# Spreading the output product's four matmuls between the last projection products of a step

## The chip, the cores and the metric

The kernel runs on one core of one Trainium2 chip. The metric is the device time of one execution in microseconds (us); a run of the kernel is timed several times and the median is given. The engines of the core are TensorE (PE in the profile; PEld is its weight load), VectorE (DVE), ScalarE (ACT), GpSimd (POOL) and SyncE (SP, which issues transfers). Each works through its own list of instructions in order and waits on semaphores for the others.

## The reference

The input x has 128 rows (S) of 256 tokens (R) of 256 channels, all float32. Two layers follow each other, each adding its result to x. Layer 0, which the change is in, works on the group-normalized x:

```python
gate = jax.nn.sigmoid(msa_repr @ gate_proj).reshape(bs, s, r, head, c)
q, k, v = jnp.split(msa_repr @ qkv_proj, 3, axis=-1)
sim = jnp.einsum('nsqhc,nskhc->nshqk', q, k) * scale
sim = jax.nn.softmax(sim, axis=-1)
sim = sim + bias
attend = jnp.einsum('nshqk,nskhc->nsqhc', sim, v) * gate
out = attend.reshape(bs, s, r, cm) @ out_proj
```

Each of the 128 rows has its own attention over its 256 tokens, with 8 heads of 32 channels. The bias comes from the pair representation and is the same for all rows. The last line is the output product that the change moves. Layer 1 normalizes again and applies an attention with 4 heads within a band of 16 tokens.

## The kernel before, in words

Channels lie on the partitions (two halves of 128) and tokens along the free dimension. The kernel first reads x and the pair representation for the statistics and the bias, then runs layer 0 row by row, then layer 1.

In layer 0 the order on TensorE, ScalarE and VectorE is the order of the program text, written out by hand (`tc.manual_schedule`); only GpSimd's and the transfers' order is left to the framework's scheduler. The loop runs over steps s = 0 to 128. One step holds, on TensorE: the scores of row s for the first four heads (`scores(s, 0)`, tile sim, L640), the sums of the exponentials of row s-1 (`sum_heads`, zs, L681, and the bias product bv, L667), the scores of the other four heads, the weighted values of row s-1 (`attend`, av, L667), a `stretch` of projections for later rows, and the output product of row s-1 (`by_channel`, po, L513).

A stretch computes two of the four projections q, k, v, g for a pair of rows: q and k in an even step, v and g in an odd one, from s = 0 to 125. The first row pair's stretches stand ahead of the loop. Each projection is made by seven half-size products in the manner of Strassen (class `Seven`). Products 1, 5, 2, 3, 6, 7, 4 of the two projections f and g alternate. The products 3, 6, 7 and 4 build on each other in a projection's PSUM bank: 6, 7 and 4 accumulate in half 0, and ScalarE takes a snapshot of it after 6 and after 7 (`take("6")` L623, `take("7")` L625, each 128x256 to the tile mid) and of the whole bank at the end (`take("34")`, L627). A product may not write on until the snapshot before it has been taken. For v a product is two matmuls of 128 columns (L614), for q, k and g one of 256 columns (L610). A float32 matmul shows as two matmul records in the profile.

The snapshots are added up on GpSimd (L630, L631). GpSimd also makes the sums of rows that the products 4 to 7 read (`sum_rows`, L584 to L587, tile ts), once per row pair. VectorE normalizes (xt L503, xn L573), adds up exponentials (both, L657), and makes the reciprocal of the gated denominators (d, L696 and L697), from which the operand of the output product results:

```python
nc.vector.tensor_tensor(t, bv0, z, ALU.mult)
nc.vector.tensor_tensor(t, av, t, ALU.add)
at = row.tile([P, 2, R], F32, tag="at", name=f"at{s}")
nc.vector.tensor_tensor(at, t, d, ALU.mult)
```

`finish` then adds po to the row (o, L723). Scores, projections and output product share a ring of five PSUM banks; zs, bv and av have one bank each.

Of the kernel before, what the change touches and what calls it, by code (L numbers as in the profile page):

```python
# [15 lines left out]
P = 128  # L16
# [23 lines left out]
def conv_preact_kernel(  # L40
# [14 lines left out]
    nc = tc.nc  # L55
# [16 lines left out]
    def bank(which, name):  # L72
        pool, tag, bufs = ring[which]
        return pool.tile([P, 2, R], F32, tag=tag, name=name, bufs=bufs)

    def proj_bank(name):
        return bank("proj", name)
# [30 lines left out]
    out_sb = const.tile([P, 2, C], F32, name="out_sb")  # L108
# [399 lines left out]
    def by_channel(w, col, xn, name, ring="proj"):  # L508

        ps = bank(ring, name)  # L510
        for m in range(2):
            for kt in range(2):
                nc.tensor.matmul(  # L513
                    ps[:, m, :], lhsT=w[:, kt, col + m * P : col + (m + 1) * P], rhs=xn[:, kt, :],
                    start=(kt == 0), stop=(kt == 1),
                )
        return ps
# [14 lines left out]
    def rows(ap, s0, n):  # L532
        return ap[s0 : s0 + n].rearrange("s h p q -> p s h q")
# [5 lines left out]
    with ExitStack() as both:  # L539
# [11 lines left out]
        with ExitStack() as lay0:  # L551
            row = lay0.enter_context(tc.tile_pool(name="row0", bufs=2))
            att = lay0.enter_context(tc.tile_pool(name="att0", bufs=2))
            st, hd, outs = {}, {}, {}
# [5 lines left out]
            def normal(s):  # L560
                if s >= S:
                    return
                g, k = ROWS[s]
                if k == 0:
                    load(g + 1)
                xt = row.tile([P, 2, R], F32, tag="xt", name=f"xt{s}", bufs=6)
                turned(xt, xgs[g], k)
                st[s] = {"xt": xt}
                i, r = divmod(s, 2)
                if r == 0:  # L570
                    xns[i] = row.tile([P, 4, R], F32, tag="xn", name=f"xn{i}")
                for half in range(2):
                    nc.vector.tensor_scalar(  # L573
                        xns[i][:, 2 * r + half, :], xt[:, half, :],
                        mean0[:, half : half + 1], rstd0[:, half : half + 1],
                        op0=ALU.subtract, op1=ALU.mult,
                    )

            def sum_rows(i):

                if 2 * i >= S:
                    return
                x, t = xns[i], row.tile([P, 4, R], F32, tag="ts", name=f"ts{i}", bufs=1)
                nc.gpsimd.tensor_tensor(t[:, 0], x[:, 2], x[:, 0], ALU.subtract)  # L584
                nc.gpsimd.tensor_tensor(t[:, 1], x[:, 3], t[:, 0], ALU.subtract)
                nc.gpsimd.tensor_tensor(t[:, 2], x[:, 3], x[:, 2], ALU.subtract)
                nc.gpsimd.tensor_tensor(t[:, 3], t[:, 1], x[:, 1], ALU.subtract)  # L587
                tss[i] = t
# [44 lines left out]
            def scores(s, half):  # L633
                i, r = divmod(s, 2)
                q, k = res["q", i], res["k", i]
                sims = [sim_bank(f"sim{s}_{half}_{j}") for j in range(4)]
                for kt in range(2):
                    for j in range(4):
                        p0 = D0 * j
                        nc.tensor.matmul(  # L640
                            sims[j][:, kt, :],
                            lhsT=k[p0 : p0 + D0, 2 * r + half, kt * P : (kt + 1) * P],
                            rhs=q[p0 : p0 + D0, 2 * r + half, :],
                            start=True, stop=True,
                        )
                ex = att.tile([P, 4, 2, R], F32, tag="ex", name=f"ex{s}_{half}", bufs=4)
                both = att.tile([P, 4, R], F32, tag="both", name=f"both{s}_{half}")
                hd[s, half] = (ex, both)

                for j in range(4):  # L650
                    nc.scalar.activation(ex[:, j], sims[j], AF.Exp, scale=1.0 / math.sqrt(D0))  # L651
# [21 lines left out]
            def sum_heads(s):  # L673
                if s < 0:
                    return
                zs = ps_av.tile([P, 2, R], F32, tag="z", name=f"zs{s}")
                bv0 = ps_av.tile([P, 2, R], F32, tag="bv", name=f"bv{s}")
                for half in range(2):
                    both = hd[s, half][1]
                    for j in range(4):  # L680
                        nc.tensor.matmul(  # L681
                            zs[D0 * j : D0 * (j + 1), half, :], lhsT=ones[:, 0:D0], rhs=both[:, j, :],
                            start=True, stop=True,
                        )
                products(bv0, s, lambda h, kt: bias_sb[:, kt, h, :])
                hd[s] = bv0
                return zs
# [27 lines left out]
                nc.vector.tensor_tensor(at, t, d, ALU.mult)  # L715
                st[s]["at"] = at

            def finish(s, po):
                g, k = divmod(s, XG)
                if k == 0:  # L720
                    outs[g] = big1.tile([P, XG, 2, R], F32, tag="o", name=f"o{g}")
                o = outs[g]
                nc.vector.tensor_tensor(o[:, k], po, st[s]["xt"], ALU.add)  # L723
                if k % 2 == 1:
                    for half in range(2):
                        nc.vector.bn_stats(out=stats1[:, half, s // 2, :], in_=o[:, k - 1 : k + 1, half, :])
                if k == XG - 1:
                    nc.sync.dma_start(out=rows(x1, g * XG, XG), in_=o)
                    outs.pop(g)
                st.pop(s)  # L730

            def stretch(names, i):

                if 2 * i >= S:
                    return
                f, g = (Seven(w, i) for w in names)


                for p in (f, g):
                    p.open()  # L740
                    p.product(1)
                    p.product(5)
                    p.take("15")
                twos = proj_bank(f"p2{names}{i}")
                two = row.tile([P, 2, R], F32, tag="two", name=f"two{names}{i}")
                f.product(2, twos[:, 0, :])
                g.product(2, twos[:, 1, :])
                nc.scalar.copy(two, twos)  # L748
                for p in (f, g):
                    p.product(3)  # L750
                    p.product(6)
                    p.take("6")
                for p in (f, g):
                    p.product(7)
                    p.take("7")
                for p in (f, g):
                    p.product(4)
                    p.take("34")
                for n, p in enumerate((f, g)):
                    p.add(two[:, n, :])  # L760


            with tc.manual_schedule(engines={mybir.EngineType.PE, mybir.EngineType.Activation, mybir.EngineType.DVE}):
                for s in range(2):
                    normal(s)
                sum_rows(0)
                stretch("qk", 0)
                for s in range(2, 4):
                    normal(s)
                stretch("vg", 0)  # L770
                sum_rows(1)
                for s in range(S + 1):
                    if s < S:
                        scores(s, 0)
                    zs = sum_heads(s - 1)
                    join_tiles(s, 0, 0)
                    divide(s - 1, zs)
                    if s % 2 == 0 and s < S:
                        e = res["g", s // 2]
                        nc.scalar.activation(e, e, AF.Exp, scale=-1.0)  # L780
                    if s < S:
                        scores(s, 1)
                    z = hd[s - 1, "z"][0] if s > 0 else None
                    attend(s - 1)
                    for half, j in ((0, 2), (1, 0), (1, 2)):
                        join_tiles(s, half, j)
                    least(s - 1, z)
                    if s == S - 1:
                        most1 = join_most(st1, stats1, 1)
                        load1(0)  # L790
                        load1(1)
                    stretch(("qk", "vg")[s % 2], s // 2 + 1)
                    normal(s + 4)
                    if s % 2 == 1:
                        sum_rows((s + 3) // 2)
                    if s > 0:
                        finish(s - 1, by_channel(out_sb, 0, st[s - 1]["at"], f"po{s - 1}"))
            mean1, rstd1 = channel_columns(st1, most1, stats1, 1)
        banks0.close()

# [3 lines left out]
        with ExitStack() as lay:  # L804
# [3 lines left out]
            st, hd, outs = {}, {}, {}  # L808
# [362 lines left out]
```

## Time and profile before

| what | value |
|---|---|
| time, median of 3 runs | 3365.25 us (3362.61 to 3367.5) |
| span of the profiled execution | 3361.1 us |
| PE busy | 3268.2 us (97%), 37193 matmul records |
| PEld busy | 2493.9 us (74%) |
| DVE busy | 2685.3 us (80%) |
| ACT busy | 1818.2 us (54%) |
| POOL busy | 1254.2 us (37%) |
| po (L513): first and last start | 236.6 and 2183.3 us, 1024 records, median 379 ns |
| PE idle before po, until at was ready | 12.1 us, 3 times |

An engine's busy time is the sum of its instructions' durations as the profile gives them. Layer 0's loop runs from about 220 to 2185 us, so that its 128 steps take most of the time. In the profile's timeline each line has the start and the duration in us, the engine, the line of the kernel, the operation, what it writes and reads, and the shape; in square brackets stands the idle time of the engine ahead of it, and whom it waited for.

### The profile page before, as it was taken

How to read it: one execution, taken by the hardware profiler on the slowest of the kernel's cores; microseconds unless marked ns; L12 is line 12 of the kernel's file. 1: busy time of each engine (PE TensorE's matmuls, PEld its weight loads, DVE VectorE, ACT ScalarE, POOL GpSimd, SP SyncE). 2: the span in 40 equal slices, each digit the busy share in tenths (PEclk: the TensorE clock that was granted, in tenths of full speed). 3: DMA queues.
4: the chain of work that ended last, by engine and by line, in shares of the span. 5: the costliest groups of instructions: out<-in, count | busy, mean ns of one | idle time of the engine just before them, and what ended most of it. 6: DMA issues, size and time to landing. Idle time of an engine off the chain costs nothing.

```text
span 3361.1 us, 86626 instructions
## 1 busy us (share of the span) xinstructions
PE 3268.2 (97%) x37193; PEld 2493.9 (74%) x37193; DVE 2685.3 (80%) x3794; ACT 1818.2 (54%) x3866; POOL 1254.2 (37%) x1135
## 2 busy tenths in 40 slices
PE   6799999999999999999999999899999999999997
PEld 4566767666776767676767666588888888888886
DVE  4748988888888889888988888857777777777776
ACT  4566666666666666666666666444444444444442
POOL 3034344434444443444344434233333333333332
PEclk8899999999999999999999999999999999999998
DMA  9922111111111111111111111012222222222211
GB/s 383 410 69 58 45 39 33 39 33 33 39 36 35 33 39 33 39 33 39 33 39 33 39 33 27 20 33 62 55 65 64 53 64 64 60 57 64 64 52 46
DMA packets 346327, 209.35 MB, mean 62 GB/s; under 512 B 273608, under 2 KB 339152, under 8 KB 339664
## 3 DMA queue, kind: packets, MB, share of 16 engines
q1 hardware_dynamic: 345040, 201.37, 20.6%
q8 instruction: 294, 4.82, 0.6%
q0 software_dynamic: 752, 2.36, 0.2%
q14 instruction: 97, 0.79, 0.1%
q10 hardware_dynamic: 144, 0.00, 0.0%
HBM read 136.59 MB, written 67.11 MB: 61 GB/s over the span
## 4 chain that ended last, share of the span: by engine, by line
PE 92%; DMA 4%; DVE 2%; ACT 1%; issue 0%; ACTq 0%; SPq 0%; POOL 0%; DVEq 0%
PE sim L640 8%; PE p1v L835 7%; PE av L667 7%; PE 1po L513 7%; PE po L513 7%; PE p1q L513 7%; PE p1k L513 7%; PE bv L667 6%; PE pg L610 6%; PE pk L610 6%; PE pq L610 5%; PE pv L614 5%; PE zs L681 4%; PE 1sim L856 3%; PE 1avz L888 2%; DMA xs<-in_x_dram 2%
## 5 line engine op out<-in xcount | busy, mean ns | idle before, releaser
L651 ACT ACTIVATE ex<-sim 128x512 f32<-128x512 f32 x1024 | 528.8, 604 | 370.1 <-PE sim L640 370.1
L913 DVE RECIPROCAL 1rz<-1z 128x512 f32<-128x512 f32 x128 | 427.7, 3341 | 174.2 <-ACT 1z L911 174.2
L657 DVE TENSOR_TENSOR both<-ex 128x512 f32<-128x512 f32 x512 | 463.1, 944 | 113.0 <-ACT ex L651 113.0
L866 POOL TENSOR_TENSOR 1p<-1ex,seen 128x768 f32<-128x768 f32 x128 | 233.6, 1825 | 735.9 <-ACT 1ex L864 735.9
L697 DVE RECIPROCAL d<-d 128x512 f32<-128x512 f32 x128 | 429.2, 3353 | 4.4
L640 PE MATMUL sim<-q,k 32*128 32x256 f32 x4096 | 294.7, 400 | 1.1 <-ACT ex L651 1.1
L827 ACT ACTIVATE 1q<-p1q,bqk 128x256 f32<-128x256 f32 x256 | 107.2, 470 | 344.9 <-PE p1q L513 344.9
L630 POOL TENSOR_TENSOR v<-v,twovg 128x256 f32<-128x256 f32 x64 | 56.7, 886 | 592.8 <-ACT twovg L748 592.8
L640 PEld LDWEIGHTS sim<-q,k 32*128 32x128 f32 x4096 | 185.9, 184 | 102.2 <-issue 49.4
L513 PE MATMUL po<-at,out_sb 128*128 128x256 f32 x1024 | 245.6, 383 | 12.1 <-DVE at L715 12.1
L667 PE MATMUL av<-ex,v 128*32 128x256 f32 x4096 | 247.5, 382 | 0.0
L513 PE MATMUL 1po<-1at,w_out_t 128*128 128x256 f32 x1024 | 242.0, 390 | 5.0 <-DVE 1at L915 5.0
L513 PE MATMUL p1q<-xn,w_in_t 128*128 128x256 f32 x1024 | 243.7, 381 | 2.0 <-DVE xn L493 1.1
L667 PE MATMUL bv<-bias_sb,v 128*32 128x256 f32 x4096 | 244.5, 379 | 0.0
L513 PE MATMUL p1k<-xn,w_in_t 128*128 128x256 f32 x1024 | 241.9, 379 | 0.0
L835 PEld LDWEIGHTS p1v<-w_in_t,xn 128*64 128x64 f32 x4096 | 222.2, 137 | 21.6 <-issue 21.6
L835 PE MATMUL p1v<-w_in_t,xn 128*64 128x128 f32 x4096 | 237.9, 274 | 0.0
L513 PEld LDWEIGHTS 1po<-1at,w_out_t 128*128 128x128 f32 x1024 | 191.1, 192 | 54.9 <-ACT 1z L911 23.9
L513 PEld LDWEIGHTS po<-at,out_sb 128*128 128x128 f32 x1024 | 196.5, 192 | 40.5 <-issue 7.7
L513 PEld LDWEIGHTS p1q<-xn,w_in_t 128*128 128x128 f32 x1024 | 195.2, 191 | 29.4 <-issue 1.3
L513 PEld LDWEIGHTS p1k<-xn,w_in_t 128*128 128x128 f32 x1024 | 194.6, 190 | 26.5
L493 DVE TENSOR_SCALAR xn<-yg,mean,rstd 128x256 f32<-128x256 f32 x256 | 94.0, 410 | 138.7 <-PE p1v L835 138.7
(226 smaller groups left out, 6690.9 us busy)
## 6 DMA issues: line engine op xcount, KB each, us to landing
pr<-in_L_conv_pair_repr_dram SPq DMA_DIRECT2D x32, 1024.0 KB, 22.9
x<-o SPq DMA_DIRECT2D x64, 512.0 KB, 2.8
yg<-x SPq DMA_DIRECT2D x64, 512.0 KB, 4.2
out_dram<-1o SPq DMA_DIRECT2D x256, 128.0 KB, 4.1
xg<-in_x_dram SPq DMA_DIRECT2D x252, 128.0 KB, 3.1
xs<-in_x_dram SPq DMA_DIRECT2D x15, 2048.0 KB, 21.8
xs<-in_x_dram SPq DMA_DIRECT2D x2, 1024.0 KB, 17.9
qkv_sb<-in_L_conv_qkv_proj_dram POOLq DMA_DIRECT2D x4, 192.0 KB, 12.6
```

The source lines that it names most:

```text
L513: nc.tensor.matmul(ps[:, m, :], lhsT=w[:, kt, col + m * P : col + (m + 1) * P], rhs=xn[:, kt, :], start=(kt == 0), stop=(kt == 1),)
L610: nc.tensor.matmul(out, lhsT=stationary(self.w, n), rhs=moving, start=first, **flags)
L614: nc.tensor.matmul(out[:, cols], lhsT=moving[:, cols], rhs=stationary(self.w, n), start=first and t2 == 0, **flags)
L640: nc.tensor.matmul(sims[j][:, kt, :], lhsT=k[p0 : p0 + D0, 2 * r + half, kt * P : (kt + 1) * P], rhs=q[p0 : p0 + D0, 2 * r + half, :], sta ...
L651: nc.scalar.activation(ex[:, j], sims[j], AF.Exp, scale=1.0 / math.sqrt(D0))
L657: nc.vector.tensor_tensor(both[:, j : j + 2], ex[:, j : j + 2, 0, :], ex[:, j : j + 2, 1, :], ALU.add)
L667: nc.tensor.matmul(to[D0 * j : D0 * (j + 1), half, :], lhsT=v[:, 2 * r + half, c0 : c0 + D0], rhs=weights(4 * half + j, kt), start=(kt == ...
L681: nc.tensor.matmul(zs[D0 * j : D0 * (j + 1), half, :], lhsT=ones[:, 0:D0], rhs=both[:, j, :], start=True, stop=True,)
L697: nc.vector.reciprocal(d, d)
L835: nc.tensor.matmul(ps[KB * half : KB * (half + 1), b, :], lhsT=xn[:, kt, KB * b : KB * (b + 1)], rhs=w_in_t[:, kt, 2 * C + P * half : 2 * ...
L866: nc.gpsimd.tensor_tensor(p.rearrange("p j (r c) -> p (j r) c", c=WROW)[:, :, 0 : 2 * WSTEP] .rearrange("p r (t c) -> p r t c", c=WSTEP)[: ...
L913: nc.vector.reciprocal(rz, z)
```

## The change

The output product of row s-1 stood as a block of four matmuls after the stretch. It becomes a generator, `output(s)`, that gives out one matmul at a time. `stretch` gets the row as a third argument and takes one of the four matmuls between product 7 of f and product 7 of g, one between product 4 of f and product 4 of g, and the last two at its end. It is meant to give TensorE work in the places where a product waits for ScalarE's snapshot. Where there is no stretch (the last steps) the four stand together as before. `finish` reads the bank from the row's state. The computation is unchanged, and so is the number of instructions that compute.

```diff
-            def finish(s, po):
+            def finish(s):
+                if s < 0:
+                    return
+                po = st[s]["po"]
...
-            def stretch(names, i):
-
+            def output(s):
+
+                if s < 0:
+                    return
+                st[s]["po"] = proj_bank(f"po{s}")
+                for m in range(2):
+                    for kt in range(2):
+                        nc.tensor.matmul(
+                            st[s]["po"][:, m, :], lhsT=out_sb[:, kt, m * P : (m + 1) * P],
+                            rhs=st[s]["at"][:, kt, :],
+                            start=(kt == 0), stop=(kt == 1),
+                        )
+                        yield
+
+            def stretch(names, i, s):
+
+                po = output(s)
                 if 2 * i >= S:
+                    for _ in po:
+                        pass
                     return
...
-                for p in (f, g):
-                    p.product(7)
-                    p.take("7")
-                for p in (f, g):
-                    p.product(4)
-                    p.take("34")
+
+                for n, what in ((7, "7"), (4, "34")):
+                    f.product(n)
+                    f.take(what)
+                    next(po, None)
+                    g.product(n)
+                    g.take(what)
+                for _ in po:
+                    pass
...
-                    stretch(("qk", "vg")[s % 2], s // 2 + 1)
+                    stretch(("qk", "vg")[s % 2], s // 2 + 1, s - 1)
                     normal(s + 4)
                     if s % 2 == 1:
                         sum_rows((s + 3) // 2)
-                    if s > 0:
-                        finish(s - 1, by_channel(out_sb, 0, st[s - 1]["at"], f"po{s - 1}"))
+                    finish(s - 1)
```

The program's order on GpSimd, which the scheduler makes, changes too in the odd steps. Before: row sum L584, v plus mid, g plus mid, row sums L585, L586, L587. After: v plus mid, L584, L586, L585, g plus mid, L587.

More of the change, by code (lines that the diff above doesn't have):

```diff
@@ L766, in conv_preact_kernel @@
                 sum_rows(0)
-                stretch("qk", 0)
+                stretch("qk", 0, -1)
                 for s in range(2, 4):
                     normal(s)
-                stretch("vg", 0)
+                stretch("vg", 0, -1)
                 sum_rows(1)
```

## The prediction

> **What bounds the kernel now.** I read the page first (engine shares, then the chain that ended last), then the timeline of one step of layer 0 on the PE, weight-load, ScalarE and VectorE rows, then the windows view of two steps.
>
> ```profile
> PE 3268.2 (97%) x37193; PEld 2493.9 (74%) x37193; DVE 2685.3 (80%) x3794; ACT 1818.2 (54%) x3866; POOL 1254.2 (37%) x1135
> ...
> PE 92%; DMA 4%; DVE 2%; ACT 1%; issue 0%; ACTq 0%; SPq 0%; POOL 0%; DVEq 0%
> ```
>
> TensorE sets the time: 97% busy, 92% of the chain. But a matmul's end in the profile is modelled, so "busy" can hide loss. What counts is the distance between the starts of successive matmuls. The timeline of TensorE (start, duration, both in us) at the end of one q/k stretch:
>
> ```profile
> 1017.33 0.59 PE L610 MATMUL pk<-xn,sums_k 128*128 128x256 f32 x2
> 1017.76 0.59 PE L610 MATMUL pk<-ts,sums_k 128*128 128x256 f32 x2
> 1018.19 0.59 PE L610 MATMUL pq<-ts,sums_q 128*128 128x256 f32 x2
> 1018.81 0.70 PE L610 MATMUL pk<-ts,sums_k 128*128 128x256 f32 x2
> 1019.35 0.66 PE L610 MATMUL pq<-ts,sums_q 128*128 128x256 f32 x2
> 1019.98 0.70 PE L610 MATMUL pk<-ts,sums_k 128*128 128x256 f32 x2
> 1020.51 1.89 PE L513 MATMUL po<-at,out_sb 128*128 128x256 f32 x8
> 1022.33 1.15 PE L640 MATMUL sim<-q,k 32*128 32x256 f32 x16
> ```
>
> The first three starts are 0.43 apart. From product 7 of q (1018.19) on they are 0.62, 0.54, 0.63 and 0.53 apart: 2.32 us for four products where 4 x 0.433 = 1.73 would do. **0.59 us is lost per q/k step without an idle line to show it.** Why, is in the weight-load and ScalarE rows:
>
> ```profile
> 1018.01 0.37 PEld L610 LDWEIGHTS pq<-ts,sums_q 128*128 128x128 f32 x2
> 1018.81 0.30 PEld L610 LDWEIGHTS pk<-ts,sums_k 128*128 128x128 f32 x2 [0.43 <-ACT midk L623]
> 1019.31 0.30 PEld L610 LDWEIGHTS pq<-ts,sums_q 128*128 128x128 f32 x2 [0.20 <-issue]
> 1019.97 0.30 PEld L610 LDWEIGHTS pk<-ts,sums_k 128*128 128x128 f32 x2 [0.37 <-ACT midk L625]
> 1020.30 1.70 PEld L513 LDWEIGHTS po<-at,out_sb 128*128 128x128 f32 x8
> ```
>
> ```profile
> 1018.39 0.37 ACT L623 COPY midk<-pk 128x256 f32<-128x256 f32 x1 [0.49 <-PE pk L610]
> 1018.82 0.38 ACT L625 COPY midq<-pq 128x256 f32<-128x256 f32 x1
> 1019.55 0.37 ACT L625 COPY midk<-pk 128x256 f32<-128x256 f32 x1 [0.35 <-PE pk L610]
> 1020.05 0.58 ACT L627 COPY q<-pq 128x512 f32<-128x512 f32 x1
> ```
>
> Product 7 of k may start only when ScalarE has copied product 6 out (1018.39 + 0.37 = 1018.76); it starts at 1018.81, its weights not loaded ahead. So do the next two: each waits for a copy of its own half bank, with only one product of the other projection between. The output product po, whose weights were loaded 0.21 early (1020.30 against 1020.51), waits for none of these copies. The v/g step shows the same: product 7 of v starts at 1033.57, po at 1035.95, 2.38 us where 2 x 0.447 + 2 x 0.433 = 1.76 would do: **0.62 lost.**
>
> po's operand is long there, and the engine behind it is the next fullest (VectorE timeline, then the windows view of two steps):
>
> ```profile
> 1016.59 0.69 DVE L715 TENSOR_TENSOR at<-t,d 128x512 f32<-128x512 f32 x1
> ...
> 1025.25 0.67 DVE L657 TENSOR_TENSOR both<-ex 128x512 f32<-128x512 f32 x1
> 1026.23 0.69 DVE L696 SCALAR_TENSOR_TENSOR d<-g,z 128x512 f32<-128x512 f32 x1 [0.31 <-ACT z L694]
> ```
>
> ```profile
> 1013.00:1043.74 30.74, 30.62 (x314) 21.50 (x310) 26.55 (x33) 19.18 (x41) 12.57 (x12) 1.00 0.14 36
> ```
>
> at ends at 1017.28, 3.2 us before po. Two steps last 30.74, VectorE works 26.55 of them (fourth figure).
>
> **What the Trainium skill says.** "Perfetto Trace Analysis", section Tensor Engine Instruction, says that the reported start comes after the semaphore wait and that the end is an estimate from the size. The trace agrees: a matmul that waited is simply longer (0.70 against 0.59) and no idle time stands before it. "TensorE: Matmul & The Clock Gate", in the section on the array of 16 sub-arrays, says that the queue can pull weight loads ahead of running matmuls while ScalarE and VectorE are strict FIFO; loads that wait for nothing are 0.18 to 0.21 early here, those of the waiting products not at all. "SBUF — State Buffer", section SBUF: two separate sides, says that VectorE and GpSimd share a port pair which one instruction holds to its end while the other blocks. The trace agrees at L573: a 128x256 xn takes 0.36 at best and 1.35 where a GpSimd sum runs.
>
> **The change, part by part.** No instruction is added or dropped on TensorE: po's four matmuls move up. Order now: f7, g7, f4, g4, po x4. Changed: f7, po, g7, f4, po, g4, po, po. Every waiting product gets a second matmul between itself and the copied one. With f7 = 0 in the q/k step and a pitch of 0.433: po 0.43, g7 0.87, f4 1.30, po 1.73, g4 2.17, po 2.60, po 3.03, scores 3.55 (a switch to scores costs 0.09 more, 1022.33 - 1020.51 = 1.82 against 1.73). Before, scores stood at 1022.33 - 1018.19 = 4.14. Now each wait, with weights wanted 0.2 ahead:
> - g7 needs the copy of g6, which ends at 0.57 (as before), plus 0.05 to be seen (1018.76 to 1018.81); wanted at 0.67. In the v/g step it ends at 0.63 (1034.20), seen at 0.68, wanted at 0.68: just in time.
> - f4 needs the copy of f7: end 0.59, start 0.63, end 1.00, seen 1.05; wanted at 1.10.
> - g4 needs the copy of g7: g7 ends 1.46, copy 1.50 to 1.87, seen 1.92; wanted at 1.97.
> - The next scores reuse the banks of f and g: their last copies end at about 2.5 and, for g, 2.17 + 0.59 + 0.04 + 0.58 = 3.38, before 3.55.
> - po needs at: ready at 1017.28 - 1018.19 = -0.91, wanted at 0.23, 1.14 to spare; v/g: -1.20 against 0.25, 1.45 to spare. If at were late, everything behind po on TensorE would wait, products and the next scores.
>
> So all the lost time closes, though three margins are 0.00 to 0.10. The interleaving happens in steps 1 to 125, 62 of them q/k, 63 v/g: 62 x 0.59 + 63 x 0.62 = 75.6 us. I leave off 3 us for margins that miss now and then. Layer 1 and the start are untouched. 3365.25 - 72.6 = **3292.7 us**.
>
> **What shorter steps do elsewhere.** VectorE: from d at 1010.92 to the end of both at 1025.92 it works without pause, 15.00 us; that step shrinks to 15.31 - 0.59 = 14.72, so d comes 0.3 late in the v/g step, hidden by the 1.45 above. The v/g step has pauses for it (over 2 us before d), and a pair asks 26.6 to 27.2 of 29.5. GpSimd: its order shifts. The sum v+mid now stands ahead of three row sums (L584, L586, L585: 0.74, 0.73, 1.18), g+mid behind them. So g+mid ends about 4.2 to 4.6 after the scores start, instead of 2.4 (1038.91 + 1.28 - 1037.77). ScalarE's exponential of g (L780, at +3.65 before) waits for it, 0.55 to 0.95 late, and the second half's exponentials are queued behind: they started at +4.96, now 5.3 to 5.7, and take 2.06. Nobody wants them before 7.7 (the second projection's first product) and ScalarE itself had no other work until 7.91. Cost: nothing. But g+mid then runs where VectorE wants the port for d (+3.90): d 0.3 to 0.7 late, up to 1.4 if the next GpSimd sum also gets in first. The spare time of at in that step is 1.14: 0 in the likely case, 0.3 or more in the worst.
>
> **Rivals.**
> - *Margins miss.* The copies come a little late for g7 and g4, and each again exposes its weight load, 0.10 (0.53 against 0.43): 125 x 0.2 = 25 us, 3318. For it: the zero margin in the v/g step. Against: durations here repeat to 0.01 or 0.02.
> - *VectorE becomes the bound in the q/k steps:* at comes late through the port and TensorE stands before po for about 0.6: 62 x 0.6 = 37, 3330. For it: g+mid moving onto d. Against: 1.14 to spare.
> - *It all comes back elsewhere:* the scores or the exponentials set the step and it stays 15.4: 3365. Against: ScalarE works only 19.18 of 30.74.
> - *Slower:* po's pieces close no gap, and the two extra islands of po expose their own weights, 2 x 0.11 x 125 = 27: 3393. Against: po's weights wait for nothing today.
>
> **How the numbers follow.** Forecast 0.72, missed margins 0.13, VectorE 0.09, no change 0.03, slower 0.03. Time 3293. Low: every gap closes and 0.05 more a step, 3284. High: missed margins and a part of the VectorE case, 3325; outside is about 0.15. Faster by over 0.2% (6.7 us) holds in the first three: 0.94; same 0.03; slower 0.03.
>
> **What would show it.** In the changed profile the products and po stand 0.43 to 0.45 apart from f7 to the scores, weight loads of g7, f4, g4 begin ahead of their matmuls, no product of 0.70 remains there, and a pair of steps lasts about 29.5 instead of 30.74. The mean of pk<-ts and pg<-ts (406 and 405 ns) falls to about 380. Wrong if a wait of po for at (12.1 us, 3 times before) grows to dozens of times, if loads still start with their matmuls, or if the pair stays above 30.

## The result and the profile after

The changed kernel takes 3289.65 us, median of 4 runs (3287.92 to 3290.82), against 3364.79 for the kernel before: a ratio of 0.9776, with a 95% interval of 0.9759 to 0.9793. It is faster by 75 us, and the forecast of 3293 was 3 us too high.

From the page of the changed kernel, the engines and the chain that ended last:

```profile
PE 3204.8 (97%) x37193; PEld 2506.1 (76%) x37193; DVE 2732.7 (83%) x3794; ACT 1820.0 (55%) x3866; POOL 1250.6 (38%) x1135
...
PE 93%; DMA 3%; DVE 3%; ACT 0%; issue 0%; SPq 0%; DVEq 0%; ACTq 0%
```

The share of TensorE is 97% as before; its instructions are the same 37193, and 63 us of "busy" are gone. That is the loss that hid in long matmuls. Busy time counts overlapping instructions once, so it is not the sum of their durations: po's 1024 records last 384 ns in the mean and make 287.4 us of it. The span is 74 us shorter; the other 10 us were idle time of TensorE, 93 us before and 83 now. The end of a q/k stretch, in the timeline of TensorE (start and duration in us):

```profile
1046.33 0.59 PE L610 MATMUL pq<-ts,sums_q 128*128 128x256 f32 x2
1046.76 0.59 PE L742 MATMUL po<-at,out_sb 128*128 128x256 f32 x2
1047.19 0.59 PE L610 MATMUL pk<-ts,sums_k 128*128 128x256 f32 x2
1047.63 0.59 PE L610 MATMUL pq<-ts,sums_q 128*128 128x256 f32 x2
1048.06 0.59 PE L742 MATMUL po<-at,out_sb 128*128 128x256 f32 x2
1048.49 0.59 PE L610 MATMUL pk<-ts,sums_k 128*128 128x256 f32 x2
1048.92 1.03 PE L742 MATMUL po<-at,out_sb 128*128 128x256 f32 x4
1049.88 0.50 PE L640 MATMUL sim<-q,k 32*128 32x256 f32 x4
```

All starts are 0.43 or 0.44 apart, no product is 0.66 or 0.70 long, and the scores follow 3.55 after product 7 of q (4.14 before). The weight loads and the snapshots of the same stretch, in the timelines of PEld and ScalarE:

```profile
1046.55 0.41 PEld L742 LDWEIGHTS po<-at,out_sb 128*128 128x128 f32 x2
1046.98 0.41 PEld L610 LDWEIGHTS pk<-ts,sums_k 128*128 128x128 f32 x2
1047.45 0.37 PEld L610 LDWEIGHTS pq<-ts,sums_q 128*128 128x128 f32 x2
1048.28 0.41 PEld L610 LDWEIGHTS pk<-ts,sums_k 128*128 128x128 f32 x2
...
1049.88 0.31 PEld L640 LDWEIGHTS sim<-q,k 32*128 32x128 f32 x7 [0.33 <-issue]
```

```profile
1046.53 0.37 ACT L623 COPY midk<-pk 128x256 f32<-128x256 f32 x1 [0.49 <-PE pk L610]
1046.96 0.37 ACT L625 COPY midq<-pq 128x256 f32<-128x256 f32 x1
1047.83 0.37 ACT L625 COPY midk<-pk 128x256 f32<-128x256 f32 x1 [0.49 <-PE pk L610]
1048.26 0.59 ACT L627 COPY q<-pq 128x512 f32<-128x512 f32 x1
1049.12 0.59 ACT L627 COPY k<-pk 128x512 f32<-128x512 f32 x1 [0.28 <-PE pk L610]
```

Each of the three loads for products (L610) starts 0.18 to 0.21 ahead of its matmul (1046.98 for 1047.19), and the snapshot it needs has ended just before: 1046.90, 1047.33 and 1048.20, that is 0.08 to 0.12 ahead of the load. The copies last as long as before; only what stands between is new.

The windows view of two steps (length, then busy time of PE, PEld, DVE, ACT and POOL) answers to the one of before, 30.74 long with TensorE busy for 30.62:

```profile
1018.81:1048.34 29.53, 29.53 (x312) 21.63 (x311) 27.66 (x33) 19.19 (x40) 12.93 (x12) 1.00 0.14 37
```

Two steps are 1.21 shorter. So are all: in 60 pairs of steps of each trace, the distance from the first scores of a step to those of the next is 15.31 (q/k) and 15.44 (v/g) before, 14.71 and 14.82 after, and repeats within 0.003. What one step loses may thus be multiplied by the number of steps. VectorE is busier (27.66 against 26.55 in these windows). One place where it loses time is beside GpSimd's sum of g with its snapshots (g plus mid). On GpSimd, VectorE and ScalarE, the start of a step whose scores begin at 1035.17:

```profile
1037.89 1.72 POOL L631 TENSOR_TENSOR g<-g,midg 128x512 f32<-128x512 f32 x1
```

```profile
1039.07 1.09 DVE L696 SCALAR_TENSOR_TENSOR d<-g,z 128x512 f32<-128x512 f32 x1 [0.59 <-ACT z L694]
...
1044.92 0.69 DVE L715 TENSOR_TENSOR at<-t,d 128x512 f32<-128x512 f32 x1
```

```profile
1039.65 1.06 ACT L803 ACTIVATE g<-g 128x1024 f32<-128x1024 f32 x1 [0.68 <-POOL g L631]
```

g plus mid ends at 1039.61, 4.44 after the scores (2.4 before), and the exponential of g starts 0.04 later, at +4.48 instead of +3.65. d starts on time, but ends 0.55 after the GpSimd sum and takes 1.09 for 0.91. at ends at 1045.61, still ahead of po, but 0.94 before po's weight load (1046.55) where the prediction had 1.14: the longer d has used up most of the difference.

### The profile page after: what moved, and what is told of

The parts are those of the page before. It is cut to its first block, busy times and chain, and to the rows that moved or that the text cites. A ratio compares the mean times of both kernels' runs of the same rounds, so it can differ in the third digit from the quotient of the medians.

```text
span 3287.4 us, 86502 instructions
## 1 busy us (share of the span) xinstructions
PE 3204.8 (97%) x37193; PEld 2506.1 (76%) x37193; DVE 2732.7 (83%) x3794; ACT 1820.0 (55%) x3866; POOL 1250.6 (38%) x1135
## 4 chain that ended last, share of the span: by engine, by line
PE 93%; DMA 3%; DVE 3%; ACT 0%; issue 0%; SPq 0%; DVEq 0%; ACTq 0%
PE sim L640 8%; PE p1v L857 7%; PE av L667 7%; PE 1po L513 7%; PE po L742 7%; PE p1q L513 7%; PE p1k L513 7%; PE bv L667 7%; PE pv L614 6%; PE pq L610 5%; PE pk L610 5%; PE pg L610 5%; PE zs L681 4%; DMA xs<-in_x_dram 3%; PE 1sim L878 3%; PE 1avz L910 2%
## 5 line engine op out<-in xcount | busy, mean ns | idle before, releaser
L657 DVE TENSOR_TENSOR both<-ex 128x512 f32<-128x512 f32 x512 | 483.7, 984 | 77.8 <-ACT ex L651 77.8
L742 PE MATMUL po<-at,out_sb 128*128 128x256 f32 x1024 | 287.4, 384 | 12.1 <-DVE at L715 12.1
L630 POOL TENSOR_TENSOR v<-v,twovg 128x256 f32<-128x256 f32 x64 | 72.8, 1137 | 551.1 <-ACT twovg L768 551.1
L742 PEld LDWEIGHTS po<-at,out_sb 128*128 128x128 f32 x1024 | 187.0, 193 | 34.1 <-issue 7.7
```

The costliest lines, as they stand in the source:

```text
L657: nc.vector.tensor_tensor(both[:, j : j + 2], ex[:, j : j + 2, 0, :], ex[:, j : j + 2, 1, :], ALU.add)
L742: nc.tensor.matmul(st[s]["po"][:, m, :], lhsT=out_sb[:, kt, m * P : (m + 1) * P], rhs=st[s]["at"][:, kt, :], start=(kt == 0), stop=(kt == 1),)
```

## The experiments

All keep every operation and change places alone; one of them changes nothing but GpSimd's order. The diffs are against the changed kernel, with its loop over the products written out. GpSimd's order, where the scheduler makes it, came out in some of the runs as in the kernel before (one gap filled at product 7, the block, two after the products 7) and in the others as in the changed kernel. Each was timed beside the kernel before (3363.0 to 3364.5 us in these sets).

**One gap filled, product 7's or product 4's.** The first leaves g's product 4 right behind f's, the second g's product 7 right behind f's:

```diff
-                for n, what in ((7, "7"), (4, "34")):
-                    f.product(n)
-                    f.take(what)
-                    next(po, None)
-                    g.product(n)
-                    g.take(what)
+                f.product(7)
+                f.take("7")
+                next(po, None)      # first run only
+                g.product(7)
+                g.take("7")
+                f.product(4)
+                f.take("34")
+                next(po, None)      # second run only
+                g.product(4)
+                g.take("34")
```

> Only the gap of product 7 is filled: f7, po, g7, f4, g4, po, po, po. Theory (each gap is its own wait for a snapshot, and takes one matmul to fill): g4 waits again for the snapshot of g7, 0.19 us plus 0.10 us of exposed weight load a step, the other half of the loss stays away. 3290 + 125 x 0.29 = 3326 us; one product of 0.70 us a step is left, g's product 4. Rival A (one matmul moved up anywhere is enough to let ScalarE catch up): 3290. Rival B (what helps is that po, and with it o on VectorE, comes earlier): po ends 0.3 us later than in the changed kernel, but the step would follow VectorE, not the gaps.

> Only the gap of product 4 is filled: f7, g7, f4, po, g4, po, po, po. Theory: g7 waits again for the snapshot of g6, 0.19 us (q/k) or 0.24 (v/g), and the weights of g7 and f4 are exposed, 0.10; g4 waits no longer. 3290 + 62 x 0.29 + 63 x 0.35 = 3330 us. The sum of what the two single gaps recover is the whole change: (3365 - 3326) + (3365 - 3330) = 74. Rival A: 3290, as above.

Measured: 3323.84 us (ratio to before 0.9882, 0.9866 to 0.9899) and 3333.07 (0.9907, 0.9891 to 0.9924). Of 3363.17 the two recover 39 and 30 us, 69 together; the whole change recovers 75. They are 2 and 3 us from the theory, and one matmul anywhere (3290) is refuted. Of the 6 us between 69 and 75, some 4 lie in the q/k steps of the second run: there po starts 0.50 after product 4 of q (1007.88 and 1008.38) instead of 0.43. In the kernel before this falls into the wait of product 4 of k and does not count. The product that still waits is the one named. TensorE and the weight load of the first run:

```profile
1032.59 0.59 PE L610 MATMUL pq<-ts,sums_q 128*128 128x256 f32 x2
1033.22 0.70 PE L610 MATMUL pk<-ts,sums_k 128*128 128x256 f32 x2
1033.75 0.59 PE L742 MATMUL po<-at,out_sb 128*128 128x256 f32 x2
```

```profile
1033.21 0.30 PEld L610 LDWEIGHTS pk<-ts,sums_k 128*128 128x128 f32 x2 [0.43 <-ACT midk L625]
```

0.63 from f's product 4 to g's, and 0.53 to po: 0.20 of waiting and 0.10 of exposed load, and the load waits for L625, the snapshot of product 7. In the second run the same line stands at product 7 and names L623, the snapshot of product 6:

```profile
1007.35 0.30 PEld L610 LDWEIGHTS pk<-ts,sums_k 128*128 128x128 f32 x2 [0.43 <-ACT midk L623]
```

**The whole of po as one block ahead of f7.**

```diff
+                for _ in po:
+                    pass
                 f.product(7)
                 f.take("7")
-                next(po, None)
                 g.product(7)
```

(and no matmul of po in or behind the products that follow.)

> All four matmuls of po as a block before f7, none between the products and none at the end. Theory: only g7's wait goes; f4 and g4 wait for the snapshots, and with nothing behind g4 the scores of the next step wait for the last copy of g's bank, some 0.6 us. About 1.0 us a step more than the changed kernel and 0.4 more than the kernel before: 3400 to 3415 us. Rival B (the earlier place of po is what helps): po is earliest here, 3290 or below.

Measured: 3384.7 us (1.0065, 1.0048 to 1.0082), slower than before as the theory says, though by 15 us less than the low end of what was expected. The rival, that po helps by being early, is refuted: it is earliest here. The v/g step in the timeline of TensorE:

```profile
1011.94 0.61 PE L614 MATMUL pv<-sums_v,ts 128*128 128x128 f32 x4
1012.38 0.60 PE L610 MATMUL pg<-ts,sums_g 128*128 128x256 f32 x2
1013.01 0.71 PE L614 MATMUL pv<-sums_v,ts 128*128 128x128 f32 x4
1013.56 0.60 PE L610 MATMUL pg<-ts,sums_g 128*128 128x256 f32 x2
1014.08 1.44 PE L640 MATMUL sim<-q,k 32*128 32x256 f32 x16
1015.45 1.07 PE L681 MATMUL zs<-both,ones 128*32 128x256 f32 x16
```

Product 7 of g waits no longer (0.44); product 4 of v does (0.63, and 0.55 to the next). New is the last pair of lines: from the scores to zs it is 1.37 instead of 1.08, because the fourth score's bank is still being copied. ScalarE's last copies of that step:

```profile
1013.76 0.59 ACT L627 COPY v<-pv 128x512 f32<-128x512 f32 x1 [0.37 <-PE pv L614]
1014.24 0.59 ACT L627 COPY g<-pg 128x512 f32<-128x512 f32 x1
```

Read one by one, three scores start from 1014.08 to 1014.10 and the fourth at 1014.39, just behind the end of v's copy (1014.35) and long before that of g's (1014.83). The expectation had the wrong bank: with po finished ahead of the products 4, the scores stand in the banks of po and f, not of f and g. I had sized the wait at 0.6; it is 0.29 in this step. In the q/k step it is 1.66, 0.58 more, and there the wait for the bank that the finished po leaves is the longer one, until VectorE's o has read it:

```profile
1029.45 0.30 PEld L640 LDWEIGHTS sim<-q,k 32*128 32x128 f32 x4 [0.33 <-PE pq L610]
1030.05 0.73 PEld L640 LDWEIGHTS sim<-q,k 32*128 32x128 f32 x12 [0.30 <-DVE o L726]
```

o ended at 1030.00, the copy of q at 1029.71. po's bank was not in my sum.

**One matmul in each gap, or one after each product 7.** The first run has po after f7, g7, f4 and g4; the second after f7 and g7, and two at the end.

```diff
                 f.product(7)
                 f.take("7")
                 next(po, None)
                 g.product(7)
                 g.take("7")
+                next(po, None)
                 f.product(4)
                 f.take("34")
-                next(po, None)      # removed in the second run only
                 g.product(4)
                 g.take("34")
+                next(po, None)      # first run; the second has both at the end
```

> One matmul of po after each of f7, g7, f4 and g4, so only one is left behind g4. Theory: no product waits, as in the changed kernel, but g4 and its last copy come 0.43 us later; the copy is seen at 3.87 us after f7 where the fourth score wants the bank at about 3.75: 0.05 to 0.15 us a step, 3297 to 3308 us. Rival (any spreading is as good, nothing depends on the two matmuls at the end): 3290, or less since every product has more room.

Measured: 3324.78 us (0.9887, 0.9870 to 0.9903). No product waits, and still half of the gain is gone: 35 us over the changed kernel, where I expected 7 to 18. TensorE and ScalarE at the end of a stretch:

```profile
1033.73 0.59 PE L610 MATMUL pk<-ts,sums_k 128*128 128x256 f32 x2
1034.17 0.59 PE L742 MATMUL po<-at,out_sb 128*128 128x256 f32 x2
1034.69 1.44 PE L640 MATMUL sim<-q,k 32*128 32x256 f32 x16
1036.06 1.07 PE L681 MATMUL zs<-both,ones 128*32 128x256 f32 x16
```

```profile
1034.37 0.58 ACT L627 COPY k<-pk 128x512 f32<-128x512 f32 x1 [0.28 <-PE pk L610]
```

The copy that frees k's bank ends at 1034.95, 0.26 after the scores have begun, and scores to zs is 1.37 where 1.08 is usual: 0.29 a step, and 125 x 0.29 = 36 us, within 1 us of the distance to the changed kernel. I had taken the four scores to begin one after the other, so that the fourth could come 0.2 late. In the changed kernel all four start from 1049.88 to 1049.90; here three start from 1034.69 to 1034.71 and the fourth at 1035.00, so its wait counts in full.

> One matmul of po after f7 and one after g7, then f4, g4 next to each other, and two at the end. Theory (a snapshot needs two matmuls behind its product, wherever they come from, and g's last copy two before the scores): f7 0, po 0.43, g7 0.87, po 1.30, f4 1.73, g4 2.17, po 2.60 and 3.03, scores 3.55. g4's snapshot is seen at 1.92, wanted at 1.97; the last copy of g waits for f's and is seen at 3.58, where the run with one matmul in each gap puts the fourth score's need at about 3.57. 3290 to 3296 us. Rival (g4 needs a matmul of po right before it): as with the gap of product 4 open, 3324.

Measured: 3289.86 us (0.9780, 0.9764 to 0.9796), the same as the changed kernel. So it is not po that g4 needs beside it: two matmuls behind the copied product are enough, and f4 and g4 may stand next to each other. Together with the run before, this also shows that the two at the end are part of the change's gain. And GpSimd's order is in this run that of the kernel before, so the whole gain comes without the new order of GpSimd.

**GpSimd's order from the program text.**

```diff
-            with tc.manual_schedule(engines={mybir.EngineType.PE, mybir.EngineType.Activation, mybir.EngineType.DVE}):
+            with tc.manual_schedule(engines={mybir.EngineType.PE, mybir.EngineType.Activation, mybir.EngineType.DVE, mybir.EngineType.Pool}):
```

> The changed kernel with GpSimd's order taken from the program text too: v and g sums first, then the four row sums, so that g plus mid ends about 2.7 us after the scores start and ScalarE's exponential of g waits for nobody. Theory (GpSimd's later sum and the late exponential and late d are hidden): the same 3290 us within 5. Rival (the 0.7 us by which ScalarE waits for g plus mid comes back as time, once in two steps): 63 x 0.3 to 0.7, 3246 to 3271 us.

Measured: 3290.18 us (0.9781, 0.9765 to 0.9797). ScalarE's line in this run:

```profile
1039.72 1.08 ACT L803 ACTIVATE g<-g 128x1024 f32<-128x1024 f32 x1
```

The scores begin at 1036.07 there, so the exponential of g is back at +3.65 and waits for nobody, and d takes 0.76. VectorE is busy for 2675.7 us in the whole kernel, where the changed kernel has 2732.7: GpSimd's order alone makes this difference. The time does not move: the late exponential and the slow d of the changed kernel are hidden.

**po ahead of its operand.** The first matmul of po goes before product 3.

```diff
                 nc.scalar.copy(two, twos)
+                next(po, None)
```

> The first matmul of po stands before product 3, 2.7 us after the stretch starts, ahead of its operand at (done at 3.5 in q/k steps, 3.3 in v/g steps by the kernel before). Theory (TensorE works in order, so a late operand of po holds up all behind it): it starts about 0.15 us after at, and the next matmul's weights are exposed: 1.07 us lost in q/k and 0.82 in v/g steps, 3290 + 62 x 1.07 + 63 x 0.82 = 3408 us (3390 to 3425). Rival (at is not what matters, or the wait takes up slack that the step has elsewhere): 3290 to 3330.

Measured: 3417.03 us (1.0161, 1.0144 to 1.0178). at and the first po of a v/g step, in the timelines of VectorE and TensorE:

```profile
1022.06 0.69 DVE L715 TENSOR_TENSOR at<-t,d 128x512 f32<-128x512 f32 x1
```

```profile
1022.89 0.67 PE L742 MATMUL po<-at,out_sb 128*128 128x256 f32 x2 [0.26 <-DVE at L715]
1023.40 0.61 PE L614 MATMUL pv<-sums_v,xn 128*128 128x128 f32 x4
```

po starts 0.14 after at ends and product 3 behind it is held up with it. The wait shows as idle time of 0.26, though po is 0.42 behind where the product before it would allow (1022.04 + 0.43 = 1022.47). In q/k steps po is 0.91 late:

```profile
1005.58 1.03 PE L610 MATMUL p2qk<-xn,qkv_sb 128*128 128x256 f32 x4
1007.35 0.67 PE L742 MATMUL po<-at,out_sb 128*128 128x256 f32 x2 [0.74 <-ACT twoqk L768]
```

The profile names ScalarE's copy twoqk here, but that copy (end 1007.23) and at (end 1007.21) end together. In the v/g step po starts while the copy twovg still runs (1022.68 to 1023.26), so po does not need it, and at is what it waits for in both. The sum comes out as forecast for another reason than in the expectation: less in the v/g steps, but this order too leaves only one matmul of po behind g4 and pays the 0.29 of the scores' bank. With the exposed load, 62 x (0.91 + 0.08 + 0.29) + 63 x (0.42 + 0.07 + 0.29) = 128 us on 3290.

## Why the prediction was right

- *What bounds the kernel.* TensorE, by lost starts without an idle line. Right in the main: 63 us of its busy time went with the same instructions, and only 10 us of idle time, and the runs with one gap filled lose 0.20 + 0.10 at the product that was named, waiting for the snapshot that was named. The reading of the weight loads was too plain: in the v/g step of the kernel before, those of g behind products of v are 0.10 to 0.11 early, not 0.18 to 0.21, and v's product 4 waits although its load starts 0.15 ahead of it (1034.64 for 1034.79).
- *Order of starts from f7 to the scores.* Right to the hundredth: scores at 3.55 in the q/k step, and two steps of 29.53.
- *Margins of 0.00 to 0.10.* They held: the three loads are early, and the length of the steps repeats in 60 pairs. That of 0.00 held too (in the v/g step the copy ends at 1032.22, the load starts at 1032.27 and the matmul at 1032.47). So the 3 us taken off for misses were not needed, and are what the forecast was too high by: 75.6 us was the sum without them, 75.1 to 75.6 was measured.
- *The next scores reuse the banks of f and g.* Right in that the last copy is done in time; this is a tight point of the change, since with 0.43 less behind g4 it costs 35 us.
- *Shorter steps elsewhere.* VectorE's d in the v/g step came 0.28 later than z allows (0.3 forecast), g plus mid ended at +4.44 (4.2 to 4.6), the exponential was 0.83 late (0.55 to 0.95). The late sum and exponential cost nothing, as the run with GpSimd's order from the program text shows, and the v/g step, where d was late, reached its forecast length all the same. That g plus mid ended in its range is luck in part: the row sum L585 took 0.73 where 1.18 was taken, and g plus mid itself 1.72 where 1.28 was. Other sizes were off: in the q/k step d was to come 0.3 to 0.7 late; it started on time and took 0.18 longer. at had 0.94 to spare there instead of 1.14. VectorE was to need 26.6 to 27.2 in a pair of steps and was busy for 27.66 in the pair shown.
- *Signs of being right or wrong.* The mean of pk<-ts and pg<-ts fell from 406 and 405 ns to 381 and 379 (about 380 forecast). po waits for at as before, 12.1 us in 3 waits.
- *Rivals.* A copy that comes too late and a late at both exist as costs: the runs with one gap filled or one matmul behind g4 pay for the first, the run with po ahead of its operand for the second. The changed order stays clear of both. VectorE as the bound, no change and slower did not come about; the orders that are slower than before are the block ahead of f7 (3385) and po ahead of its operand (3417).

Not tried: whether the remaining 0.1 lost at each first product of a stretch and at each change to the scores can be won back.

## What to carry to other kernels

Look at the distance between the starts of matmuls, not at idle time: a product that waits for a copy of its own bank loses the wait and the hidden weight load with hardly an idle line. Independent matmuls from elsewhere in the step could fill such places here for nothing, if they are counted out: as many behind each product as its copy takes, and some left for the last copy, whose bank the next stage wants. Moving them can also change which bank the next stage gets, as in the run with the block. Check first that their operand is ready at the new place, since everything behind them on the engine waits for it.

## What the runs showed of the hardware that was not expected

The four scores, which use different rows of the array (32*128 in the profile), start within 0.02 us of each other, so all their banks are wanted at nearly the same moment: one bank that is copied 0.26 us after the start of the first delays what follows the group by 0.29.

A weight load was not early where the array's shape changes. In the changed kernel the first load of the scores starts with its matmul (1049.88 both) behind po, though the profile names nothing that it waits for, and the last po lasts 0.96 to it for two matmuls, where 0.87 would do. The load of zs behind the scores does the same (1050.95 both), while that of bv, which has the shape of zs, is 0.21 early in the kernel before (1024.08 for 1024.29). The prediction counted this 0.09 as it found it; no run here isolates its cause.
